# Attention before a mixture of experts: the second head pair's products in one run at the head of the next slot, ten score tiles in a row, router steps and sine products in other places

## The chip, the core and the metric

The kernel runs on one core of a Trainium2 chip. TensorE (PE) multiplies matrices and transposes, writing into PSUM; VectorE (DVE) and ScalarE (ACT) do the elementwise work and empty PSUM; GpSimd (POOL) does index work and indirect transfers; SyncE (SP) issues most DMA transfers. Each of them works through its own list in order, and they wait for each other on semaphores. The metric is the device time of one execution in microseconds (us), as a median of runs. Everything is in float32, except a small mask in bfloat16.

## The reference

Input x has the shape 8 x 1024 x 512 (batch, tokens, features). Two blocks follow each other, each on a layer norm of its input and each added to it. The second is a mixture of experts: a router (x @ Wr, softmax over 8 experts, the best 2, at most 160 tokens per expert and batch entry) and two matrix products per expert with a relu between. The change does not touch the experts. The first block is an attention with 16 heads of 32 features, whose queries, keys and values are sines and cosines of angles:

```python
theta_q = xh / (1.0 + jnp.abs(w_q)) + b_q + t * phi_q
sin_q, cos_q = lookup_sin_cos(theta_q)
Q = jnp.concatenate([cos_q, sin_q], axis=-1)          # the same for K
theta_v = xh / (1.0 + jnp.abs(w_v)) + b_v
V = cos_v + sin_v
scores = jnp.einsum('bqhd,bkhd->bhqk', Q, K) / scale
scores = jnp.where(causal, -jnp.inf, scores)
attn = jax.nn.softmax(scores, axis=-1)
out = jnp.einsum('bhqk,bkhd->bqhd', attn, V).reshape(B, S, D)
theta_out = out / (1.0 + jnp.abs(w_out)) + b_out
return cos_o + sin_o
```

`lookup_sin_cos` reads a table of 2048 steps with linear interpolation. A head's query and key vectors have 64 numbers (32 cosines and 32 sines).

## The kernel before

Attention is done in 32 slots, the loop `for n in range(NCK)` from line 1736. Slot n is batch entry b = n // 4 and feature block c = n % 4: 128 features, that is 4 heads, taken as two pairs of heads. A schedule written out by hand sets the order on PE, ACT, DVE and SP: the order in which Python emits instructions is the order on each of these engines. Most helpers are generators, and `some(k, gens)` and `rest(gen)` (lines 730 and 736) run so many steps of them, or all.

Scores. `scores` (line 675) makes ten tiles per pair of heads: three for the first 512 queries (h = 0) and seven for the second (h = 1). One tile holds the scores of 128 keys against 512 queries for both heads of the pair, two banks of PSUM; the two tiles of two blocks share one, and one tile per half is 256 wide. Line 684 are its matmuls (64 rows deep, the two heads side by side in the rows of the array), line 698 adds a causal mask to the tiles on the diagonal, and line 704 is the exponential on ACT, out of PSUM into an SBUF tile `e`. There are as many `e` buffers as one pair has tiles.

Products. `attend` (line 710) multiplies the exponentials of a tile with the values (line 718: 128 deep, 64 columns wide) and sums over the tiles in `av`, one bank; three steps for h = 0 and seven for h = 1. After the last step DVE copies `av` to `av_sb` (line 726). `turn` (line 742) transposes `av_sb` (PE, line 216), and DVE divides by the sums (lines 753 and 755).

Angles. For a slot two later, `qk_pre` (line 508) transposes x on PE (line 216) and DVE takes the angles out of PSUM in four steps (line 525). `angle` (line 437) shifts them on DVE; `both` (line 588) is two squares and two absolute values on ACT (lines 442 and 585); `qk_sin` (line 592) takes two sines on ACT (lines 594 and 445), behind a load of ACT's sine table, and the next exponential is behind a load of the other table. `qk_post` (line 599) makes the cosine products and the sine products on DVE (line 448, on `qk_c` and on `qk_r`), each followed by four DMAs from SP (line 609) that put them into the `qk` tiles of the two pairs. `v_pre` and `v_post` do the same for the values without transfers (lines 626, 631, 438, 448); `o_pre` and `o_post` for the attention's output (lines 647, 438, 448, 658, and the statistics of the next layer norm in line 661, together called `residual`). `layernorm1` normalizes the batch entry to come on DVE.

Router. `router` (line 787) is a generator for a finished batch entry; its steps are spread by hand over slots c = 0 to 3 of the next one. `next_rows` normalizes two tiles of rows on DVE and stores them, `features` transposes them on PE into a PSUM tile that DVE empties (line 838), `sums` multiplies by Wr (lines 858 and 875) and DVE empties it (lines 880 and 882); then come the choice of experts, and the places in the experts' lists. `route_on(k)` runs one step in slots with c = k.

PSUM. The pool `ps_s` has three buffers of two banks, given out in turn to score tiles, turns, `qk_pre`, and the router's `features`, `sums` and places. Whoever asks for the fourth waits until the first is emptied. `av` has two buffers of one bank. [...]

The order in one slot (away from the first and last): three steps of the second pair's h = 1 products of the slot before; in c = 1 `qk_pre`, `v_post`, a router step and `angle`; five score tiles of the first pair; the residual, the absolute values and the values' square; the last four steps of the products; the other five tiles; the second pair's turn of the slot before and `o_pre`; three steps of the first pair's products; sines; cosine products; seven steps of products; two score tiles of the second pair; the first pair's turn; sine products; three more tiles with the output's square before the last two; `qk_pre` in c = 1, 2, 3 (the router's start in c = 0); the second pair's h = 0 products; five tiles; the two squares.

Of the kernel before, what the change touches and what calls it, by code (L numbers as in the profile page):

```python
# [74 lines left out]
def preln_attn_moe_kernel(  # L75
# [424 lines left out]
    def load_base(n):  # L500
        if n < NCH:
            rest(make_base(n))
            return
        p = qkt.tile([P, 2, S], F32, name="qk_base")
        nc.sync.dma_start(p, base_d[n % NCH])
        bases[n] = p
# [157 lines left out]
    def tiles_of(h):  # L664


        def block(kb, at=0):
            q0 = max(512 * h, kb * P)
            return kb, q0, 512 * (h + 1) - q0, at

        d = 4 * h
        full = [[block(kb)] for kb in range(d + 1)]
        return full + [[block(d + 1), block(d + 3, 3 * P)], [block(d + 2)]]
# [36 lines left out]
    def attend(n, pr, h, es, halves):  # L710

        vt = v_tiles[n % 2]
        av = ps_av.tile([P, 512], F32, name="av")
        tiles = tiles_of(h)
        for i, parts in enumerate(tiles):
            for kb, q0, w, at in parts:
                for a in range(2):
                    nc.tensor.matmul(  # L718
                        av[a * 64 : (a + 1) * 64, q0 - 512 * h :],
                        lhsT=vt[:, kb, 2 * pr + a, :], rhs=es[i][:, a, at : at + w],  # L720
                        start=kb == 0, stop=i + 1 == len(tiles),
                    )
            if i + 1 == len(tiles):
                av_sb = avp.tile([P, 512], F32, name="av_sb")
                q = 2 * (n % NCH) + pr
                nc.vector.tensor_scalar(av_sb, av, inv_o[:, q : q + 1], None, ALU.mult)
                halves.append(av_sb)
            yield

    def some(count, *gens):  # L730

        for gen in gens:
            while count and next(gen, 0) is None:
                count -= 1

    def rest(gen):
        got = None
        for got in gen:
            pass
        return got  # L740
# [247 lines left out]
    def part(gen):  # L988

        for name in gen:  # L990
            if name is not None:
                return
            yield

    def keep(box, gen):
        for box[0] in gen:
            yield
# [82 lines left out]
    def find_rows(i):  # L1080

        js = slice(chunks[i][1], chunks[i][1] + 2 * chunks[i][2])
        lo, hi = REACH[i]
        nc.vector.tensor_scalar(
            source[:, :, js], meta[:, :, js, 0], float(hi * S), float(lo * S),
            ALU.min, ALU.subtract,
        )
# [542 lines left out]
    def experts_begin():  # L1630

        for name, bufs in (("gp", 2), ("w1p", 3), ("t1p", 3), ("xep", 1), ("tmp_p", 2)):
            pools[name] = to_end.pool(name, bufs, reuse_waits="tile", **right)
        for k in range(AHEAD):
            load_ahead(k)
        yield from start(first_gather, first_parts)
        mix_w1(0, 0)
# [76 lines left out]
    NCK = B * NCH  # L1714
# [10 lines left out]
    pairs, v_st = qk_first()  # L1725
# [5 lines left out]
    last = None  # L1731
    o_st = route = first_rows = None
    begin = False
    place, angles, residual = [None], iter(()), iter(())
    first_gather = gather(0)
    for n in range(NCK):
        more, late = n + 1 < NCK, last is not None
        b, c = divmod(n, NCH)
        if n == NCK - 1:
            to_inputs.close()  # L1740
            first_rows = experts_begin()
        pos_n = trig.tile([P, S], F32, name="o_p")
        if n == NCK - 2:
            find_rows(0)
            next(first_gather)
        if late:
            e11, halves1, pos = last
        es, halves = [[], []], [[], []]

        products = [attend(n, 0, h, es[h], halves[0]) for h in range(2)]
        if late:
            products.insert(0, attend(n - 1, 1, 1, e11, halves1))
        ahead = [scores(pairs[0], h, es[h]) for h in range(2)]
        v_box = [None]
        asides = [keep(v_box, v_pre(n + 1))] if more else [first_rows]
        if b == 0 and c in (1, 2):
            asides.append(layernorm1(1, c - 1))
        elif c == 0 and 0 < b < B - 1:  # L1760
            asides.append(layernorm1(b + 1, 1))
        elif c == 3 and b + 2 < B:
            asides.append(layernorm1(b + 2, 0))
        def route_on(slot):
            if c == slot and route is not None:
                next(route)

        def with_asides(count):
            for _ in range(count):
                some(1, *ahead)  # L1770
                for g in asides:
                    next(g, None)


        if late:
            some(3, *products)
        route_on(1)
        route_on(2)
        if c == 2 and route is not None:
            asides.append(part(route))  # L1780
        if n == 0:
            some(2, *ahead)
        if n == 0 or begin:

            qk_st = rest(qk_pre(n + 1))
            if begin:
                v_post(n, v_st)
                next(route)
            angle(*qk_st)
            angles = keep(place, both(qk_st))  # L1790
            if begin:
                load_base(n + 2)

        if begin:
            some(5, *ahead)
        else:
            with_asides(5)
        rest(residual)
        for _ in range(2):
            route_on(1)  # L1800
        rest(angles)
        if begin:
            rest(asides.pop(0))
            v_st = v_box[0]
        elif more:
            v_st = v_box[0]
            square(v_st[0])
        if late:
            some(4, *products)
        route_on(1)  # L1810
        route_on(1)
        with_asides(5)
        if begin:
            square(v_st[0])
        for g in asides:
            rest(g)
        if n == 0:
            magnitude(inv_o)
            base2 = make_base(2)
            next(base2)  # L1820
        if late:
            turn(1, halves1, pos)
            o_st = o_pre(n - 1, pos)
        route_on(1)
        route_on(1)
        if n == 2:
            load_b1()
        if c == 3 and b > 0:
            next(route)
            if b > 1:  # L1830
                fetch_slots(b - 2)
            if b < B - 1:
                scatter()


        some(3, *products)
        if n == 0:
            next(base2)
        if more:
            qk_st = place[0]  # L1840
            qk_sin(qk_st)
            sine(v_st[1])
        if late:
            sine(o_st[1])
        if n == 0:
            some(NTT, *products)
            rest(base2)
        if more:
            post = qk_post(qk_st)
            next(post)  # L1850
        some(NTT, *products)

        es, halves1 = [[], []], []
        ahead = [scores(pairs[1], h, es[h]) for h in range(2)]
        route_on(1)
        route_on(2)
        some(2, *ahead)
        turn(0, halves[0], pos_n)
        next_pairs = rest(post) if more else None
        some(1, *ahead)  # L1860
        if late:
            square(o_st[0])
            residual = o_post(n - 1, o_st)
        some(2, *ahead)
        begin = c == 0 and late
        if begin:
            rest(residual)
            route = router(b - 1)
            next(route)
        elif n + 2 < NCK:  # L1870
            route_on(1)
            qk_st = rest(qk_pre(n + 2))

        if c != 1:
            next(residual, None)
        if n + 2 < NCK and not begin and c != 1:
            angle(*qk_st)
        if c != 1:
            rest(residual)
        if c == 1:  # L1880
            load_mid(b)
        if c == 2 and b + 2 < B:
            load_x(b + 2)
        if more and not begin:
            v_post(n + 1, v_st)
        some(3, attend(n, 1, 0, es[0], halves1))
        route_on(1)
        if c == 1:

            angle(*qk_st)  # L1890
        some(5, *ahead)
        if n + 2 < NCK and not begin:
            angles = keep(place, both(qk_st))
            some(2, angles)
            if n + 3 < NCK:
                load_base(n + 3)
        last = (es[1], halves1, pos_n)
        pairs = next_pairs
    rest(attend(NCK - 1, 1, 1, es[1], halves1))
    turn(1, halves1, pos_n)  # L1900
    to_pairs.close()

# [57 lines left out]
```

## Time and profile before

| what | value |
|---|---|
| median of 3 runs | 3178.54 us (3177.48 to 3178.57) |
| the profiled execution | 3177.95 us |
| its span in the trace | 3176.2 us |
| PE busy, DVE busy, ACT busy | 3112.0, 2303.7, 1680.4 us |
| mean granted TensorE clock | 0.998 of full |
| L704 exponentials | 640, 569.4 us |
| L684 score matmuls | 3072, 598.3 us |
| L718 product matmuls | 3072, 523.4 us |

The span runs from the first instruction to the last. A busy engine is not always one that works: matmuls are pipelined, and their ends are modelled in the trace. A row of a timeline gives the start, the duration, the engine, the line, the operation with output and input, the form, how many were merged (x5), and in brackets how long the engine was idle before and what ended that. A row of the chain of waits gives the start, the length and what set the pace there.

### The profile page before, as it was taken

To read this page: it belongs to the slowest core of one execution; us is meant where nothing else is said; L and a number is where in the kernel's file an instruction comes from. 1 tells how busy PE (TensorE), PEld (TensorE's weight loads), DVE (VectorE), ACT (ScalarE), POOL (GpSimd) and SP (SyncE) were. 2 spreads that over 40 slices of the span, in tenths; PEclk is the share of its full clock that TensorE was granted. 3 is DMA by queue.
4 is the path that set the end of the run, shared out by engine and by line. 5 is a ranking of instruction groups with operands and counts; after the bars stand their busy time and mean duration, and the time that the engine had idled before them with its cause. 6 is when DMAs were issued, how large, how long until landed. Compare 5 with 4: busy or idle time off the path is not lost.

```text
span 3176.2 us, 52225 instructions
## 1 busy us (share of the span) xinstructions
PE 3112.0 (98%) x20086; PEld 2147.5 (68%) x20086; DVE 2303.7 (73%) x4808; ACT 1680.4 (53%) x2599; POOL 424.1 (13%) x387
## 2 busy tenths in 40 slices
PE   5999999999999999999999999999999999999998
PEld 2444444444444444689699699699698698698697
DVE  8888878887887775738658658658667767767765
ACT  7888888888888885413423423423423423423423
POOL 3000202020201122410110110110110110110010
PEclk9999999999999999999999999999999999999999
DMA  5535454555545352533523523523533433433421
GB/s 167 147 100 166 106 165 132 148 138 149 164 133 160 80 167 55 149 82 96 155 54 91 152 57 95 145 59 98 140 64 100 132 67 102 128 67 108 118 58 23
DMA packets 288552, 358.79 MB, mean 113 GB/s; under 512 B 28376, under 2 KB 199088, under 8 KB 276272
## 3 DMA queue, kind: packets, MB, share of 16 engines
q1 hardware_dynamic: 264944, 312.20, 33.7%
q0 software_dynamic: 22912, 43.22, 7.3%
q8 instruction: 160, 2.62, 0.4%
q14 instruction: 88, 0.72, 0.1%
q10 hardware_dynamic: 448, 0.02, 0.0%
HBM read 207.02 MB, written 81.22 MB: 91 GB/s over the span
## 4 chain that ended last, share of the span: by engine, by line
PE 78%; DVE 4%; ACT 1%; issue 1%; DMA 0%; SPq 0%; POOLq 0%; POOL 0%; DVEq 0%; ACTq 0%
PE ps_p L1238 30%; PE ps_p L1474 10%; PE ps_p L1537 10%; PE av L718 10%; PE ps_s L684 9%; PE ps_p L1352 8%; ACT e L704 1%; PE ps_s L216 1%; PE ps_s L698 1%; DVE qk_f L525 1%; DVE qk_r L448 0%; DMA qk<-qk_r 0%; DVE xT L838 0%; DVE xe L1174 0%; DVE xe_s L1186 0%
## 5 line engine op out<-in xcount | busy, mean ns | idle before, releaser
L704 ACT ACTIVATE e<-ps_s 128x1024 f32<-128x1024 f32 (+1 forms) x640 | 569.4, 937 | 183.5 <-PE ps_s L684 110.0
L684 PE MATMUL ps_s<-qk 64*128 64x512 f32 (+3 forms) x3072 | 598.3, 506 | 28.2 <-DMA qk<-qk_r 12.4
L718 PE MATMUL av<-e,v 128*64 128x512 f32 (+3 forms) x3072 | 523.4, 490 | 0.0
L684 PEld LDWEIGHTS ps_s<-qk 64*128 64x128 f32 x3072 | 262.3, 188 | 216.0 <-issue 106.9
L718 PEld LDWEIGHTS av<-e,v 128*64 128x64 f32 x3072 | 200.5, 137 | 283.0 <-issue 267.0
L1238 PE MATMUL ps_p<-xe,w 128*128 128x256 f32 (+1 forms) x1024 | 317.6, 433 | 1.1 <-issue 1.1
L1238 PE MATMUL ps_p<-xe_s,t 128*128 128x256 f32 (+1 forms) x1024 | 317.6, 433 | 0.0
L1238 PE MATMUL ps_p<-xe,t 128*128 128x256 f32 (+1 forms) x1024 | 317.6, 433 | 0.0
L1316 POOL DMA_INDIRECT out_dram<-y,slots x80 | 127.8, 1597 | 1261.3 <-ACT y L1311 1017.8
L769 POOL DMA_INDIRECT slot_d<-token,slot x128 | 156.6, 1223 | 997.3 <-issue 620.8
L1238 PEld LDWEIGHTS ps_p<-xe_s,t 128*128 128x128 f32 x1024 | 194.4, 190 | 81.4 <-issue 0.8
L1238 PEld LDWEIGHTS ps_p<-xe,t 128*128 128x128 f32 x1024 | 194.2, 190 | 80.4 <-issue 0.4
L1238 PEld LDWEIGHTS ps_p<-xe,w 128*128 128x128 f32 x1024 | 193.7, 190 | 79.4 <-issue 1.2
L1281 DVE TENSOR_TENSOR hid<-hid 128x256 f32<-128x256 f32 (+1 forms) x128 | 63.9, 499 | 206.4 <-ACT hid L1279 206.4
L1537 PE MATMUL ps_p<-w_t,hid 128*128 128x256 f32 x960 | 212.4, 379 | 0.8 <-DVE y L1590 0.8
L1537 PEld LDWEIGHTS ps_p<-w_t,hid 128*128 128x128 f32 x960 | 180.0, 190 | 24.4 <-DVE y L1590 1.2
L1238 PE MATMUL ps_p<-xe_s,w 128*128 128x256 f32 (+1 forms) x512 | 158.9, 433 | 0.6 <-ACT p L1254 0.6
L1352 PE MATMUL ps_p<-w,hid 128*128 128x256 f32 x640 | 142.9, 379 | 0.0
L1474 PE MATMUL ps_p<-w,hid 128*128 128x128 f32 x1104 | 141.8, 275 | 0.0
L698 PEld LDWEIGHTS <-keys_b 64*128 64x128 bf16 x1536 | 80.9, 95 | 89.7 <-issue 71.8
L1311 ACT ACTIVATE y<-y,slots 128x256 f32<-128x256 f32 (+1 forms) x120 | 65.9, 578 | 142.8 <-DVE y L1389 105.5
L1474 PEld LDWEIGHTS ps_p<-w,hid 128*128 128x128 f32 x1104 | 135.8, 192 | 2.3
(289 smaller groups left out, 5182.7 us busy)
## 6 DMA issues: line engine op xcount, KB each, us to landing
w<-in_L_ffn_W_dram SPq DMA_DIRECT2D x256, 256.0 KB, 3.4
w<-in_L_ffn_W_dram SPq DMA_DIRECT2D x64, 512.0 KB, 6.8
qk<-qk_c SPq DMA_DIRECT2D x124, 256.0 KB, 4.5
qk<-qk_r SPq DMA_DIRECT2D x120, 256.0 KB, 4.9
qk_base<-base_d SPq DMA_DIRECT2D x28, 1024.0 KB, 8.8
xn_d<-xn SPq DMA_DIRECT2D x72, 256.0 KB, 2.3
rows_d<-xg SPq DMA_DIRECT2D x70, 256.0 KB, 2.1
x_mid<-in_L_attn_x_dram SPq DMA_DIRECT2D x16, 1024.0 KB, 9.2
```

The lines of the kernel that those rows point to most:

```text
L684: nc.tensor.matmul(ps[:, a, at : at + w], lhsT=pair[r, 1, kb * P : (kb + 1) * P], rhs=pair[r, 0, q0 : q0 + w], start=at == 0, stop=not own ...
L698: nc.tensor.matmul(out_, lhsT=keys_b[r, part, :], rhs=late, start=False, stop=part == 1, skip_group_check=True,)
L704: nc.scalar.activation(e, ps[:, :, :n], AF.Exp, scale=UNIT * UNIT / math.sqrt(2 * DH))
L718: nc.tensor.matmul(av[a * 64 : (a + 1) * 64, q0 - 512 * h :], lhsT=vt[:, kb, 2 * pr + a, :], rhs=es[i][:, a, at : at + w], start=kb == 0, ...
L769: queued = nc.gpsimd.indirect_dma_start(out=slot_d[b], out_offset=bass.IndirectOffsetOnAxis(ap=idx, axis=0), in_=src, in_offset=None,)
L1238: nc.tensor.matmul(ps, lhsT=weights[:, k, :], rhs=rows[:, k, :], start=first and k == 0, stop=last and k == 1, skip_group_check=True,)
L1281: TT(g1, g3, h22, ALU.add)
L1311: nc.scalar.activation(part, part, AF.Identity, scale=meta[:, e, jj[r], 1:2].bitcast(F32))
L1316: ins = nc.gpsimd.indirect_dma_start(out=out, out_offset=bass.IndirectOffsetOnAxis(ap=meta[:, e, jj[r], 0:1], axis=0), in_=y, in_offset=No ...
L1352: nc.tensor.matmul(ps, lhsT=hid[:, k, part, cols], rhs=ws[weight][:, k, :], start=first and k == 0, stop=last and k == NHQ - 1, skip_group ...
L1474: nc.tensor.matmul(ps, lhsT=left[:, k, :], rhs=right[:, k, :], start=first and k == 0, stop=k == 3, skip_group_check=True,)
L1537: nc.tensor.matmul(ps[:, b * DC : (b + 1) * DC], lhsT=hid[:, k, part, b * P : (b + 1) * P], rhs=ws[weight][:, k, :], start=first and k == ...
```

## The change

The h = 0 products of the second pair, which stood among that pair's own scores, and the two parts of its h = 1 products, which stood around the first five score tiles of the next slot, become one run of ten steps at the head of the next slot. So each pair's ten score tiles follow each other with no products between (turns, `qk_pre` and router steps still stand among them). The rest of `angles` (absolute values; in c = 1 squares too) comes after the first three steps of that run. In c = 1 `qk_pre`, `v_post`, `angle` and the load of the next base come before the run, and the router steps that stood at the head follow it; two router steps stand after the seventh score tile instead of after the old four product steps. The sine products with their four DMAs come straight after the first pair's products, before the router steps and the turn. In c = 1 `angle` comes before the second pair's last five tiles instead of after a product run. Every computation is still there, in the same number.

```diff
@@ -1743,15 +1743,14 @@
         if n == NCK - 2:
             find_rows(0)
             next(first_gather)
-        if late:
-            e11, halves1, pos = last
         es, halves = [[], []], [[], []]
 
 
 
         products = [attend(n, 0, h, es[h], halves[0]) for h in range(2)]
         if late:
-            products.insert(0, attend(n - 1, 1, 1, e11, halves1))
+            es1, halves1, pos = last
+            products = [attend(n - 1, 1, h, es1[h], halves1) for h in range(2)] + products
         ahead = [scores(pairs[0], h, es[h]) for h in range(2)]
         v_box = [None]
         asides = [keep(v_box, v_pre(n + 1))] if more else [first_rows]
@@ -1772,12 +1771,6 @@
                     next(g, None)
 
 
-        if late:
-            some(3, *products)
-        route_on(1)
-        route_on(2)
-        if c == 2 and route is not None:
-            asides.append(part(route))
         if n == 0:
             some(2, *ahead)
         if n == 0 or begin:
@@ -1785,11 +1778,19 @@
             qk_st = rest(qk_pre(n + 1))
             if begin:
                 v_post(n, v_st)
-                next(route)
             angle(*qk_st)
             angles = keep(place, both(qk_st))
             if begin:
                 load_base(n + 2)
+        if late:
+            some(3, *products)
+            rest(angles)
+            some(7, *products)
+        for _ in range(2):
+            route_on(1)
+        route_on(2)
+        if c == 2 and route is not None:
+            asides.append(part(route))
 
         if begin:
             some(5, *ahead)
@@ -1805,11 +1806,10 @@
         elif more:
             v_st = v_box[0]
             square(v_st[0])
-        if late:
-            some(4, *products)
-        route_on(1)
-        route_on(1)
-        with_asides(5)
+        with_asides(2)
+        for _ in range(2):
+            route_on(1)
+        with_asides(3)
         if begin:
             square(v_st[0])
         for g in asides:
@@ -1849,14 +1849,14 @@
             post = qk_post(qk_st)
             next(post)
         some(NTT, *products)
-
-        es, halves1 = [[], []], []
-        ahead = [scores(pairs[1], h, es[h]) for h in range(2)]
+        next_pairs = rest(post) if more else None
+
+        es1, halves1 = [[], []], []
+        ahead = [scores(pairs[1], h, es1[h]) for h in range(2)]
         route_on(1)
         route_on(2)
         some(2, *ahead)
         turn(0, halves[0], pos_n)
-        next_pairs = rest(post) if more else None
         some(1, *ahead)
         if late:
             square(o_st[0])
@@ -1883,20 +1883,21 @@
             load_x(b + 2)
         if more and not begin:
             v_post(n + 1, v_st)
-        some(3, attend(n, 1, 0, es[0], halves1))
+        if c == 1:
+
+            angle(*qk_st)
+        some(3, *ahead)
         route_on(1)
-        if c == 1:
-
-            angle(*qk_st)
-        some(5, *ahead)
+        some(2, *ahead)
         if n + 2 < NCK and not begin:
             angles = keep(place, both(qk_st))
             some(2, angles)
             if n + 3 < NCK:
                 load_base(n + 3)
-        last = (es[1], halves1, pos_n)
+        last = (es1, halves1, pos_n)
         pairs = next_pairs
-    rest(attend(NCK - 1, 1, 1, es[1], halves1))
+    for h in range(2):
+        rest(attend(NCK - 1, 1, h, es1[h], halves1))
     turn(1, halves1, pos_n)
     to_pairs.close()
 
```

More of the change, by code (lines that the diff above doesn't have):

```diff
@@ L1885, in preln_attn_moe_kernel @@
             v_post(n + 1, v_st)
-        some(3, attend(n, 1, 0, es[0], halves1))
-        route_on(1)
         if c == 1:
             angle(*qk_st)
-        some(5, *ahead)
+        some(3, *ahead)
+        route_on(1)
+        some(2, *ahead)
         if n + 2 < NCK and not begin:
```

## The prediction

> **What bounds the kernel now.** First the page, for the engines' shares and the clock.
>
> ```profile
> PE 3112.0 (98%) x20086; PEld 2147.5 (68%) x20086; DVE 2303.7 (73%) x4808; ACT 1680.4 (53%) x2599; POOL 424.1 (13%) x387
> PEclk9999999999999999999999999999999999999999
> ```
>
> TensorE sets the time and its clock is full, so only its work and its waits count. The change stays within attention (about the first 1250 us). Next, busy time per slot of one batch, each stretch running from one ten-step product run to the next (c=0, 1, 2, 3):
>
> ```profile
> 807.51:848.14 40.63, 39.78 (x372) 19.96 (x368) 33.19 (x69) 32.02 (x34) 12.67 (x12) 1.00 0.56 156
> 848.14:887.46 39.32, 38.59 (x372) 19.13 (x368) 30.43 (x62) 32.54 (x34) 0.00 (x0) 1.00 0.67 216
> 887.46:923.70 36.24, 36.19 (x308) 17.84 (x304) 30.94 (x66) 31.89 (x33) 0.00 (x0) 1.00 0.51 146
> 923.70:959.64 35.94, 35.89 (x292) 17.61 (x289) 29.95 (x62) 31.76 (x33) 10.23 (x8) 1.00 0.38 89
> ```
>
> The columns after the stretch are its length, then PE, PEld, DVE, ACT and POOL busy. In c=2 and c=3 PE is idle for 0.05 us: hardly any wait is left to remove. ACT and DVE are busy for 30 to 32 of 36 us: little cover if their work is squeezed. The chain in such a slot:
>
> ```profile
> 923.77 7.89 PE av L718 x48
> ...
> 933.93 1.03 ACT e L704
> ...
> 937.49 2.30 PE av L718 x16
> 939.80 2.77 PE ps_s L684 x12
> ...
> 944.26 2.73 PE av L718 x12
> ...
> 951.58 3.16 PE av L718 x20
> ```
>
> The first pair's products are one run of 7.89 us; the second pair's are three, 2.30, 2.73 and 3.16. Twelve L684 matmuls are three full score tiles, so PE makes a tile in 0.93 us. The ACT piece shows three PSUM buffers just falling short: PE waits for an exponential about 0.3 us. ACT and DVE beside it:
>
> ```profile
> 912.35 4.46 ACT L704 ACTIVATE e<-ps_s 128x1024 f32<-128x1024 f32 x5 [0.33 <-PE ps_s L698]
> 916.70 2.01 ACT L585 ACTIVATE qk_c<-qk_r 128x1024 f32<-128x1024 int32 x2
> 918.60 1.15 ACT L442 ACTIVATE v_p<-v_p,split_c 128x1024 f32<-128x1024 uint16 x1
> 919.97 4.39 ACT L704 ACTIVATE e<-ps_s 128x1024 f32<-128x1024 f32 x5 [0.23 <-PE ps_s L684]
> ```
> ```profile
> 934.43 0.26 DVE L753 RECIPROCAL rec<-ps_s 128x16 f32<-128x16 f32 x1 [1.96 <-PE ps_s L216]
> 935.33 2.28 DVE L448 SCALAR_TENSOR_TENSOR qk_r<-qk_f,qk_r 128x2048 f32<-128x2048 f32 x1
> 937.71 2.73 DVE L525 SCALAR_TENSOR_TENSOR qk_f<-ps_s,inv_qk,qk_base 128x512 int32<-128x512 f32 x4
> 945.13 1.23 DVE L438 TENSOR_SCALAR qk_r<-qk_f 128x2048 int32<-128x2048 int32 x1 [2.30 <-DMA qk<-qk_r]
> ```
>
> Five tiles of exponentials take ACT 4.4 us (a full one 0.945), about PE's own 4.5 for five tiles. What lets ACT do 3.1 us of other work (L585, L442) between fives is the 3.16 us of products that PE does there. On DVE, qk_pre's evacuation (L525) holds a PSUM buffer for about 3 us after its transposes; PE has the 2.30 us product run to pass that in.
>
> **The change, part by part.** Times are on one slot, from the start of the run named.
>
> (1) One product run in place of three: 2.30+2.73+3.16 = 8.19 becomes 7.89. Gain 0.30 per slot. The Trainium skill, "TensorEngine Tiling (Array Packing)", section Key Properties, says that changing the tiling mode drains the array; products and scores differ in shape (128*64 against 64*128), and the row's price is 0.15 per cut. The same page, section PSUM Bottleneck, speaks against the change: faster tiled matmuls move the limit to evacuation. By the first rule alone the sum is -0.30 a slot; the rows say that the second governs a long run, as follows.
>
> (2) First pair's ten scores in a row. The L585 pair moves under the head's product run, but the v square (L442, 1.04 in the queue) stays between fives, and PE no longer pauses. ACT starts at 1.31 (912.35-911.04) and ends five exponentials at 5.7, the square at 6.75, then exponentials 6, 7, 8 at 7.75, 8.7, 9.65. PE unhindered would start tile 9 at 4.54+3x0.93 = 7.33; it takes the buffer of tile 6, so 7.8: 0.45 late. The turn's transposes take tile 8's buffer at 9.7 instead of 9.4: 0.3 to 0.4 more. Loss 0.85. Bounds: 0.3 (only the tile 9 wait, partly), 1.3 (the square itself waits for DVE's angle, due at about 5.7 too).
>
> (3) Second pair's scores without the 2.30 products. The buffers rotate tile 1, 2, turn, 3, 4, 5, qk_pre, 6, 7, 8. As now, tile 4 starts at 3.4, tile 5 ends at 5.25, qk_pre at 5.85. Tiles 6 and 7 follow exponentials 4 and 5, which end at 5.95 and 6.9 now (the o square and two exponentials run to 938.46, less 931.60) and end at 6.95 and 7.9. Tile 8 wants qk_pre's buffer, free at 6.05+2.73 = 8.8: it waits 0.95. End of tile 10 at 11.4; now the same work takes 944.19-931.60-2.30 = 10.3. Loss 1.1 (bounds 0.3 and 1.5). It applies where qk_pre stands there: c=1, 2, 3 up to slot 29.
>
> (4) The sine products (L448 on qk_r, 2.28) go ahead of the first pair's turn. Their time is hidden in DVE's idle 1.96 before L753; the turn's evacuation ends at 4.05 instead of 3.7, before tile 5 needs it at 4.35. The four DMAs leave some 3 us sooner, so the 2.30 us angle wait disappears, but DVE alone gains by that. No other SP transfer is passed. What is late next: router steps that used to come before them on DVE, items 5 and 6.
>
> (5) c=1 with a router (7 slots). Head: qk_pre, then 7.89 of products, cover DVE's backlog (residual 4.1, statistics and rows 4.5, after the turn's 4.05: until 12.6 of a run whose tile 10 ends at 10, so 2.6 into the head; then 2.7, 1.2 and 1.2), which now costs stalls:
>
> ```profile
> 834.97 1.99 PE L684 MATMUL ps_s<-qk 64*128 64x512 f32 x8 [0.56 <-DVE qk_f L525]
> ```
>
> From head to the turn's end now 20.7+2.30 = 23.0; after 0.9 (qk_pre) +7.9+0.7 (features) + ten tiles with three router buffers and the turn, 12.9 with about 1.1 of waits: 22.4. Gain 0.6. The two row stores move behind a qk_base load on SP; both are needed only slots later. Second pair: the logits' buffer is evacuated behind the sine products, at 3.7 instead of 1.5, and the turn needs it at 2.85: 0.85. Then features and qk_pre hold two buffers for 1.3+2.7 with no product run between; tile 8 waits 1.05; exponential waits add 0.7. Total waits about 2.7 against 1.1 now: loss 1.6. Net loss 1.0 (bounds -1 and +3).
>
> (6) c=2 with a router (7 slots). DVE is busy from v's first product at 874.89 to the second pair's turn at 888.49, 13.6 us; ten scores and a turn on PE take 10.4 after the head. With one evacuation taken out (it now comes first) DVE reaches the turn 13.7 after the head, three late. Turn 0.95, o work 1.9, evacuation 0.7 and cosine products 2.28 bring it to 19.5; the products end at 10.65+7.9 = 18.55, so their evacuation is done at 20.2, the sine products at 22.4, the router's places (0.95, before the sine products until now) at 23.3. The places, PE's first work after the products, took the buffer that the turn of the first pair is to have, at 18.55+0.6+2.1 = 21.3: 2.1 late. Net loss of the slot 0.85+1.1+2.1-0.3 = 3.8 (bounds 1.6, if DVE catches up, and 5.5).
>
> (7) c=0 gets (1) and (2): +0.55. Moved angle in c=1: DVE alone, under products.
>
> Sum: nine ordinary slots (c=3 of batches 0 to 6, c=1 and 2 of batch 0) at 0.85+1.1-0.30 = 1.65: 14.9. Slot 31 0.55; seven c=0 3.9; seven c=1 7.0; six c=2 22.8, slot 30 2.7. Total 51.8. The profiled execution is 3177.95 (span 3176.2 and 1.75 around it), 0.6 below the median of 3178.54: forecast 3177.95+52 = 3230. The feed-forward stage keeps its order.
>
> **Rivals.** *Only ACT binds* (0.17): DVE's buffers come free in time because PE is already late by exponentials. Then 0.55 for 31 slots, 17: 3195. For it: exponentials 4 and 5 nearly hold tiles 6 and 7. Against: the 0.56 wait above is DVE's with this very buffer.
>
> *DVE runs behind throughout router slots* (0.15): c=1 +3 and c=2 +5.5 give 14.9+0.6+3.9+21+36 = 76: 3254. For it: 13.7 into 10.4. Against: the eight us of products at each head let DVE catch up.
>
> *The cut's price decides, faster* (0.14): where exponentials and evacuations come free before PE asks, 31 times 0.30 is left, 9.3: 3169. It decides from the point where the waits of a slot fall below 0.30 in total, which needs tile 9 and tile 8 to be less than 0.15 late each. For it: PE's 0.93 and ACT's 0.945 are close and ACT's lag at the head is cleared. Against: the square's 1.04 is in the middle, and ends at both limits are worked from rows.
>
> *Gains and waits cancel* (0.06): about 3178.
>
> **How the numbers follow.** My case has 0.48, within 3205 to 3258. The range leaves out the faster case and most of the cancelling one: 3190 to 3258. Chances, with 0.2% (6.4 us) about what a measurement of this kernel can tell: slower 0.48+0.17+0.15 = 0.80, same 0.06, faster 0.14.
>
> **What would show it.** (1) products of 7.89 us twice per slot. (2) PE waiting for ACT e at the ninth tile and the turn. (3) a PE wait on DVE qk_f in c=2 and c=3, which is absent now, and periods of 37.6 for c=3. (4) no DVE wait for DMA qk<-qk_r. (6) DVE's first-pair turn late in c=2, period about 40. The prediction is wrong if slots keep their 36 us: then the buffers are free earlier than I reckon, or PE's 0.93 grows in long runs and leaves ACT time.

## The result and the profile after

The changed kernel takes 3250.57 us (median of 4 runs, 3249.84 to 3250.82) against 3178.01 for the kernel before beside it: a ratio of 1.0229, with a 95% interval of 1.0211 to 1.0246. It is slower by 72.6 us. That lies inside the range (3190 to 3258) and is on the forecast side, but some 21 us above the forecast of 3230. The profiled span is 3248.6 us against 3176.2, and all of the difference is in attention: the first L1238 matmul (the first product of the experts) starts at 1332.2 us instead of 1259.7.

The four slots of one batch entry, in the windows view of the changed kernel (the columns are those of the view before; c=0, 1, 2, 3). They belong to batch entry 4, those shown before to entry 5; before the change, slots of one c differ by less than 0.5 us between entries 1 to 6:

```profile
692.97:737.14 44.17, 41.12 (x372) 20.23 (x369) 33.34 (x70) 31.77 (x34) 8.94 (x10) 0.96 0.38 102
737.14:778.19 41.05, 39.01 (x372) 19.39 (x369) 29.10 (x52) 32.01 (x33) 0.00 (x0) 1.00 0.62 201
778.19:817.67 39.48, 36.51 (x308) 18.11 (x304) 32.03 (x76) 31.59 (x33) 0.00 (x0) 1.00 0.46 134
817.67:855.92 38.25, 36.36 (x293) 17.86 (x289) 30.58 (x64) 31.81 (x33) 12.06 (x9) 1.00 0.34 84
```

The slots that took 40.63, 39.32, 36.24 and 35.94 take 44.17, 41.05, 39.48 and 38.25. PE's idle time in c=3 has gone from 0.05 to 1.89 us, and the clock, the third number from the end, is not full in the first row. What PE waits for from 100 to 1330 us, in the waits view of the changed kernel (total us, times, longest):

```profile
PE ps_s L684 <- ACT e L704: 47.9, 80, 1.6
PE ps_s L216 <- DVE tmp L966: 12.2, 7, 1.8
PE ps_s L216 <- DVE prob L882: 4.4, 7, 0.6
```

Before, the first of these rows had 1.1 us, and the other two were absent. No row of this stretch names DVE qk_f, though step (3) of the prediction expected one. The chain of an ordinary slot (c=3), from the first pair's products to the product run at the next slot's head, shows what comes first instead:

```profile
654.79 7.89 PE av L718 x48
...
663.90 1.06 ACT L704
...
665.20 1.95 ACT e L704 x2
...
674.90 7.89 PE av L718 x48
```

The 1.06 us piece is no exponential. In the timeline of ScalarE it has a name:

```profile
663.90 1.28 ACT L704 ACT_TABLE_LOAD   x1 [1.47 <-PE ps_s L698]
665.20 2.56 ACT L704 ACTIVATE e<-ps_s 128x1024 f32<-128x1024 f32 x3
```

ACT is done with its sines and idle for 1.47 us, but the load of the exponential's table waits for TensorE's first score tile, and the exponential stands behind it. In a slot of c=3 of the kernel before, the load began before the products had ended (931.66) and was over at 932.67, just ahead of the end of the first score tile (932.81):

```profile
931.39 1.28 ACT L704 ACT_TABLE_LOAD   x1
932.85 2.75 ACT L704 ACTIVATE e<-ps_s 128x1024 f32<-128x1024 f32 x3 [0.17 <-PE ps_s L698]
```

Of the 33 loads that stand before an exponential, one waited for PE before the change and 31 do after it. The waits view has them as the row of L704 without a tile, first before, then after:

```profile
ACT L704 <- PE ps_s L698: 4.7, 1, 4.7
ACT L704 <- PE ps_s L698: 54.9, 31, 4.7
```

The built program shows what differs. Where the first exponential has two semaphores to wait for (PE's, and that of an earlier instruction of ACT itself), the wait for PE is an instruction of its own, and it stands in front of the table load. Where it has only PE's, the exponential carries the wait and nothing stands in front of the load.

Below, the period of a slot is the time from the start of its first pair's products to the start of the next slot's. A slot's second half runs from the start of its first pair's products to the product run at the next slot's head; a slot's head runs from that product run to its own first pair's products. So a period is the second half of one slot and the head of the next. Differences in us are ratios to the kernel before run on the same chip, times 3178, since the chips' own level differs (the kernel before took 3177 beside the first four experiments, 3190 and 3191 beside the others). The traces give a second measure, the time of the first L1238 matmul, at which attention ends. For e1 to e4 it agrees with the ratio within 2 us. For e5 to e12, on the other chips, it puts the run 2 to 8 us later than the ratio does; no trace of the kernel before was kept there, so a few us carry no weight in these runs.

### The profile page after: what moved, and what is told of

It is laid out like the page before. It is cut to its first block, busy times and chain, and to the rows that moved or that the text cites. A ratio compares the mean times of both kernels' runs of the same rounds, so it can differ in the third digit from the quotient of the medians.

```text
span 3248.6 us, 52378 instructions
## 1 busy us (share of the span) xinstructions
PE 3124.2 (96%) x20086; PEld 2153.8 (66%) x20086; DVE 2305.9 (71%) x4808; ACT 1673.2 (52%) x2599; POOL 421.1 (13%) x387
## 4 chain that ended last, share of the span: by engine, by line
PE 76%; DVE 11%; ACT 9%; issue 3%; DMA 0%; ACTq 0%; POOLq 0%; POOL 0%; DVEq 0%
PE ps_p L1238 30%; PE av L718 11%; PE ps_p L1474 10%; PE ps_p L1537 9%; PE ps_p L1352 7%; PE ps_s L684 6%; ACT e L704 6%; PE ps_s L216 1%; ACT L704 1%; DVE st_mid L661 1%; DVE qk_f L525 1%; ACT o_p L442 1%; DVE qk_r L448 1%; PE ps_s L698 1%; DVE x_mid L658 1%
## 5 line engine op out<-in xcount | busy, mean ns | idle before, releaser
L704 ACT ACTIVATE e<-ps_s 128x1024 f32<-128x1024 f32 (+1 forms) x640 | 563.8, 944 | 161.4 <-PE ps_s L698 124.9
L718 PE MATMUL av<-e,v 128*64 128x512 f32 (+3 forms) x3072 | 509.5, 488 | 0.0
L1238 PE MATMUL ps_p<-xe_s,t 128*128 128x256 f32 (+1 forms) x1024 | 317.7, 433 | 0.0
L1238 PE MATMUL ps_p<-xe,t 128*128 128x256 f32 (+1 forms) x1024 | 317.6, 433 | 0.0
L1238 PE MATMUL ps_p<-xe,w 128*128 128x256 f32 (+1 forms) x1024 | 317.6, 433 | 0.0
L1238 PEld LDWEIGHTS ps_p<-xe_s,t 128*128 128x128 f32 x1024 | 194.4, 190 | 81.4 <-issue 0.8
L1238 PEld LDWEIGHTS ps_p<-xe,t 128*128 128x128 f32 x1024 | 194.2, 190 | 80.4 <-issue 0.4
L1238 PEld LDWEIGHTS ps_p<-xe,w 128*128 128x128 f32 x1024 | 193.7, 190 | 78.2
L726 DVE TENSOR_SCALAR av_sb<-av,inv_o 128x512 f32<-128x512 f32 x128 | 95.1, 747 | 124.6 <-PE av L718 124.1
L1238 PE MATMUL ps_p<-xe_s,w 128*128 128x256 f32 (+1 forms) x512 | 158.9, 433 | 0.6 <-ACT p L1254 0.6
L698 PEld LDWEIGHTS <-keys_b 64*128 64x128 bf16 x1536 | 79.7, 95 | 90.3 <-issue 72.6
```

The source lines that it names most:

```text
L698: nc.tensor.matmul(out_, lhsT=keys_b[r, part, :], rhs=late, start=False, stop=part == 1, skip_group_check=True,)
L704: nc.scalar.activation(e, ps[:, :, :n], AF.Exp, scale=UNIT * UNIT / math.sqrt(2 * DH))
L718: nc.tensor.matmul(av[a * 64 : (a + 1) * 64, q0 - 512 * h :], lhsT=vt[:, kb, 2 * pr + a, :], rhs=es[i][:, a, at : at + w], start=kb == 0, ...
L1238: nc.tensor.matmul(ps, lhsT=weights[:, k, :], rhs=rows[:, k, :], start=first and k == 0, stop=last and k == 1, skip_group_check=True,)
```

## The experiments

**e1: the table loaded early.** A tiny exponential after the sines takes the load, away from the score tile.

```diff
             sine(o_st[1])
+        nc.scalar.activation(warm, split_c, AF.Exp)
```

> The changed kernel plus one exponential of a 128x1 tile on ScalarE straight after the sines (line 1845), so that the exponential's table is loaded there and not at the second pair's first score tile, where the load now waits for TensorE (1.47 us idle before it). Theory A (after the load, the PSUM buffer that qk_pre holds is next in line, as the forecast had it): about 0.4 us less in the second-pair half of c=2 and c=3, 0.9 in c=0, 1 at the head of c=1, together some 15 us less than the changed kernel's 3250: 3235, and waits of TensorE for DVE qk_f appear. Theory B (the late load alone sets the second-pair half): 1.2 us in each of 31 slots, 37 us: 3213.

Measured: 3227.98 us, ratio 1.0159 (1.0142 to 1.0176), 22 us less than the changed kernel. The second half of c=3 falls from 20.11 to 19.02, of c=0 from 19.34 to 18.25; of c=2 from 21.34 to 20.75 and of c=1 only from 22.56 to 22.32. So the late load costs 1.1 us where nothing else waits; theory B is right on that and wrong on the rest (22 us in all, not 37). What remains in c=3 against before is 0.83 us (19.02-7.89 = 11.13, where the same work took 10.30), and it is not what theory A says either:

```profile
658.38 2.04 PE L684 MATMUL ps_s<-qk 64*128 64x512 f32 x8
660.70 1.13 PE L684 MATMUL ps_s<-qk 64*128 64x512 f32 x4 [0.27 <-ACT e L704]
```
```profile
658.32 2.72 DVE L525 SCALAR_TENSOR_TENSOR qk_f<-ps_s,inv_qk,qk_base 128x512 int32<-128x512 f32 x4 [2.04 <-PE ps_s L216]
```

Tile 8 (the second row of PE) starts at 660.70, before DVE's evacuation of qk_pre ends at 661.04, and just after an exponential (tile 6's, at about 660.64). So it does not take qk_pre's buffer, as the prediction had it, but tile 6's: while qk_pre holds one of three buffers, two are left to circulate.

**e2: the absolute values back between the fives**, in slots that do not begin a router.

```diff
             some(3, *products)
-            rest(angles)
+            if begin:
+                rest(angles)
             some(7, *products)
```

> The changed kernel with the two absolute values (line 585, 2.0 us) back between the first pair's first five score tiles and the rest in every slot that does not begin a router. Theory A (ScalarE holds the ten-run of the first pair): 2.0 us more in 24 slots, less 0.4 because the table load no longer carries a wait there: about +38, 3288. Theory B (the wait on the table load was what the moved absolute values cost, and the ten-run has room): 1.2 us less in 24 slots, 3221.

Measured: 3286.17 us, ratio 1.0346 (1.0329 to 1.0363), 37 us more. Both theories' mechanisms are there, with A's far larger: the head of c=3 and c=0 goes from 18.14 to 20.0 or more (+1.9: ScalarE holds the ten-run), and the second half of c=3 from 20.11 to 18.96 (-1.15: the table load waits for PE in 8 of 33 places now). That these come so near to theory A's 38 is in part luck: the second halves win some 19 us in all, and in eleven of the longer heads the clock falls as well (last section), which adds some 12 us that theory A did not have. Moving the absolute values away from the ten-run is needed, and it is also what made the table load wait.

**e3: in c=1 the squares and absolute values after the first five**, as before the change.

```diff
             some(3, *products)
-            rest(angles)
+            if not begin:
+                rest(angles)
             some(7, *products)
```

> The changed kernel, but in c=1 with a router the squares and absolute values come after the first five score tiles, as before the change. Theory A (at this head ScalarE stands behind the DVE's late angle, and three buffers fill while it does): 2 to 3 us less in each of 7 slots, and where TensorE no longer idles 1.6 us its clock does not fall: together 15 to 25 less, 3225 to 3235. Theory B (DVE's evacuations hold that head, whatever ScalarE does): within 3 us of 3250.

Measured: 3252.99 us, ratio 1.0238 (1.0221 to 1.0255), no less than the changed kernel. Theory A falls. The first five tiles do go through, but then TensorE waits 2.31 us before the eighth tile for exponentials queued behind the same 4 us of ScalarE work. The work has to stand somewhere in this head, and neither of the two places tried is free.

**e4: the sine products back behind the turn.**

```diff
-        next_pairs = rest(post) if more else None
...
         turn(0, halves[0], pos_n)
+        next_pairs = rest(post) if more else None
```

> The changed kernel with the sine products back behind the first pair's turn. Theory A (forecast step 6: in c=2 and c=1 the router's buffer is emptied behind the sine products and the turn waits for it): 2.1 us less in 7 slots c=2, 0.6 to 0.9 in 7 slots c=1, about 20 less: 3230, and the waits of TensorE for DVE tmp and DVE prob go. Theory B (waits for exponentials take their place): 0 to 5 less.

Measured: 3238.93 us, ratio 1.0193 (1.0176 to 1.0210), 11 us less. The waits for DVE tmp and for DVE prob at the turn are gone, but the second half of c=2 falls by 0.87 only (21.34 to 20.47), that of c=1 not at all, and waits for exponentials grow from 47.9 to 57.4 us in the profiled execution. The remaining 5 us are falls of the clock that this execution did not have (last section). In between the theories: the wait is real, and more than half of it would have been spent on the next one.

**e5: the second pair's h = 0 products back among its scores.**

```diff
-            products = [attend(n - 1, 1, h, es1[h], halves1) for h in range(2)] + products
+            products = [attend(n - 1, 1, 1, es1[1], halves1)] + products
...
-            some(7, *products)
+            some(4, *products)
...
             v_post(n + 1, v_st)
+        some(3, attend(n, 1, 0, es1[0], halves1))
...
```

> The changed kernel with the three h = 0 product steps of the second pair back behind qk_pre, between that pair's own scores (the head's run is seven steps). Theory A (forecast step 3: tile 8 waits for the buffer that qk_pre holds): 1.1 less 0.15 for the new cut in 23 slots, 22 less than 3250: 3228. Theory B (the late table load already holds TensorE before qk_pre, so only the 0.6 us that the changed kernel's trace shows behind qk_pre can be won): 0.45 in 23 slots, 10 less: 3240.

Measured: ratio 1.0197 (1.0180 to 1.0214), 10 us less (7 by the trace), as theory B has it. The period of c=3 falls by 0.6, that of c=2 by 0.95 and that of c=1 by 0.7, while the period from c=0 to c=1, with c=1's head in it, is 0.7 longer (43.3 against 42.6, where neither kernel has a fall of the clock); the run of products in that head is shorter. Step (3)'s 1.1 is not won while the table load is late.

**e6: the last four product steps back between the first pair's fives.**

```diff
-            some(7, *products)
+            some(3, *products)
...
             square(v_st[0])
+        if late:
+            some(4, *products)
         with_asides(2)
```

> The changed kernel with the last four product steps of the head back between the first pair's two fives. Theory A (forecast step 2: ScalarE holds the ten-run, at tile 9 and at the turn): 0.85 less 0.15 for the cut in 24 slots, 17; and in 7 slots c=1 with a router, where ScalarE's angle work stands before the run, 2 to 3 more and no falls of the clock, 14 to 25: together 3208 to 3220. Theory B (the exponentials are late by as much at the next stage, so the wait moves): within 5 us of 3250.

Measured: ratio 1.0257 (1.0240 to 1.0274), 9 us more (13 by the trace). In ordinary slots theory A holds: the head of c=3 is 17.54 instead of 18.14. At c=1's head it fails badly; the period from c=0 to c=1 is 47.3 to 48.0 instead of 42.6 to 44.5:

```profile
725.16 1.22 PE L684 MATMUL ps_s<-qk 64*128 64x256 f32 x4 [2.71 <-DVE xT L838]
728.24 3.74 PE L684 MATMUL ps_s<-qk 64*128 64x512 f32 x8 [1.70 <-ACT e L704]
...
733.12 3.23 PE L718 MATMUL av<-e,v 128*64 128x512 f32 x20
```

The products at 733.12 are the cover that was taken away; without them PE reaches the scores sooner, and waits first for DVE, then for ScalarE. A part of the loss is the clock: in each of these seven heads it is half for 6.83 us, in the changed kernel for 3.41 us in three of them (last section). At this head the chain of DVE's backlog, the angle, and ScalarE's squares and absolute values sets the time in this run; TensorE's earlier start only lengthened its wait.

**e7: the values' square after the ten tiles.**

```diff
             v_st = v_box[0]
-            square(v_st[0])
         with_asides(2)
...
         with_asides(3)
-        if begin:
+        if more:
             square(v_st[0])
```

> The changed kernel with the values' square (line 442, 1.04 us in ScalarE's queue) after the ten score tiles and not between five and five. Theory A (with that square out, ScalarE's 0.945 a tile nearly keeps TensorE's 0.93): 0.7 less in 24 slots, 17: 3233. Theory B (three buffers are too few for a ten-run even so): 0 to 4 less.

Measured: ratio 1.0179 (1.0162 to 1.0196), 16 us less; but in the trace attention ends only 7 us sooner (1324.9 against 1332.2), so the total does not tell the theories apart. The slots do, for theory A. The heads of c=2, 3 and 0 lose 0.95 to 1.0 us each (18.14 to 17.19): the square in the middle was nearly the whole of TensorE's wait in the ten-run, and three buffers are enough without it. But c=2 pays 2.0 us in its second half:

```profile
621.19 1.12 PE L216 MATMUL ps_s<-ident,av_sb 64*128 64x64 f32 x16 [2.77 <-DVE tmp L966]
```

DVE is no faster, so the turn waits the longer for the buffer of the places: 2.77 us instead of 1.74. The rest of the 2.0 goes with a fall of the clock behind this wait, in all seven slots.

**e8: the sine products alone**, in the kernel before.

```diff
         some(NTT, *products)
+        next_pairs = rest(post) if more else None
...
         turn(0, halves[0], pos_n)
-        next_pairs = rest(post) if more else None
```

> The kernel before, with one part of the change alone: the sine products straight after the first pair's products. Theory A (hidden in DVE's idle 1.96 in slots without router work, but the router's buffer is emptied behind them and the turn waits for it): 1.3 more in 7 slots c=2, 0.8 in 7 slots c=1, 0 elsewhere: about +14, 3192. Theory B (there is slack enough everywhere): within 3 us of 3177.

Measured: ratio 1.0028 (1.0017 to 1.0038), 9 us more (13 by the trace), theory A: the periods of c=2 grow by 1.15, of c=1 by 0.57, and c=3 and c=0 do not change.

**e9: three losses taken out together**, the edits of e1, e4 and e7 in one kernel.

> The changed kernel with three of its losses taken out together: the early exponential of a 128x1 tile, the sine products back behind the turn, and the values' square after the ten tiles. Theory A (they are separate terms): 22 (early table) + 11 (sine) + 22 (0.95 at 23 heads; the 2 us that this square cost in c=2 came through the sine products and goes with them): 55 of the 73 us, ratio to the kernel before 1.0055. Theory B (one wait passes to the next): no more than 35 us, ratio 1.012.

Measured: ratio 1.0093 (1.0077 to 1.0108), 43 of the 73 us recovered (39 by the trace), between the theories. The periods of c=1 and c=2 come to 38.93 and 37.35, but that of c=3 only to 36.92: its second half is 19.72 here against 19.02 in e1. ScalarE is the cause. In this slot the products start at 634.25:

```profile
634.80 1.15 ACT L442 ACTIVATE v_p<-v_p,split_c 128x1024 f32<-128x1024 uint16 x1
635.97 1.28 ACT L594 ACT_TABLE_LOAD   x1
```
```profile
645.43 0.70 PE L684 MATMUL ps_s<-qk 64*128 64x256 f32 x4 [0.50 <-ACT e L704]
```

The values' square, moved behind the ten tiles by e7's edit, now stands just ahead of the sines. Their table load begins 1.72 us after the products' start instead of 0.72 (e1), the exponentials are later by nearly as much, and TensorE waits for one at the third tile, where e1 has no wait. The late table load had hidden this in e7, whose second half of c=3 is 20.11, as in the changed kernel.

**e10: the absolute values alone**, ahead of the first five tiles in the kernel before.

```diff
         if late:
             some(3, *products)
+            rest(angles)
```

> The kernel before with one part of the change alone: the absolute values (line 585) ahead of the first five score tiles. Theory A (this move makes the second pair's first exponential need two waits, one of which the table load in front of it then carries, so that the load starts only with the first score tile): 1.1 us in 24 slots, 26: ratio 1.008. Theory B (the late load comes from the ten-runs): within 0.1% of the kernel before.

**e11: the same with the early exponential** of e1.

> The same as e10_abs_alone plus the early exponential of a 128x1 tile. Theory A (the late table load is all that the moved absolute values cost): back to the kernel before, plus up to 0.2 us a slot for the added exponential: ratio 1.000 to 1.002. Theory B (absolute values ahead of the scores delay the exponentials themselves): 1.004 or more.

Measured: e10 1.0128 (1.0113 to 1.0144), e11 1.0077 (1.0061 to 1.0092). In e10 the waits view has 24 table loads that wait for PE, against one in the kernel before, and in c=2 the second half up to the h = 0 products grows from 14.08 to 15.25; in e11 it is back at 14.14. So this move by itself makes the load late, and 1.1 us is its price in the second half of such a slot; over the whole kernel, e11 takes 16 us less than e10 (13 by the trace). The rest of e10 and all of e11 is theory B's, here in e11:

```profile
780.13 2.04 PE L684 MATMUL ps_s<-qk 64*128 64x512 f32 x8 [1.40 <-ACT e L704]
```

With only three product steps ahead of the scores, squares and absolute values (4 us, until 779.08 in this slot) still run when the first tiles are ready, and TensorE waits for the exponentials behind them; the changed kernel's ten steps do cover them.

**e12: a try at a better kernel before**, two of the four product steps ahead of the first five tiles in c=1.

```diff
         if begin:
+            some(2, *products)
             some(5, *ahead)
...
-            some(4, *products)
+            some(2 if begin else 4, *products)
```

> The kernel before, but in c=1 with a router two of the four product steps stand ahead of the first five score tiles, as cover for the evacuation of features and qk_pre that now costs TensorE about 1 us there. Theory A: 0.9 less 0.15 for a new cut in 7 slots, 5 us: ratio 0.9985. Theory B (the angle work on ScalarE then meets the second five): no gain, 1.000 to 1.002.

Measured: ratio 0.9993 (0.9986 to 0.9999). In the trace the c=0 periods, which hold this head, are no shorter (40.56 to 41.22, against 40.63 to 40.87). If there is a gain it is at most 0.14%, the lower end of the interval, and the trace shows none: attention ends at 1259.9, against 1259.7 before. No version run here clearly beats the kernel before.

## Why the prediction was right, and where not

The direction and most of the size follow from what was reckoned: the second pair's products in one run win 0.30 us a slot, and what the cuts had covered comes back as waits. But the total came nearer than its parts. Steps (3) and (5) put 24 us on a wait for qk_pre's buffer that did not come (1.1 in 15 slots, 1.05 in 7), and a wait that no step looked for, the late table load, cost 22 us (e1): that these two are alike is luck. By period, summed over all slots, forecast against the traces:

| period (slots summed) | forecast, us | measured, us |
|---|---|---|
| batch 0 (4) | 5 | 8.5 |
| c=0 to c=1, with c=1's head (7) | -4 | 18.9 |
| c=1 to c=2 (7) | 15 | 12.1 |
| c=2 to c=3 (6, router batches but the last) | 22.5 | 19.5 |
| c=3 to c=0 (6) | 10 | 13.6 |
| what is left at the end | 3 | 0 |

(1) Right. Both product runs take 7.89 us. That the 0.15 per cut is the drain named in the Trainium skill, "TensorEngine Tiling (Array Packing)", section Key Properties, and not some other cost of starting a run, no run here shows. What the prediction took from the same page, section PSUM Bottleneck, is said there of matmuls that tiling has made faster, and as what may happen. Here no matmul got faster (48 products take 7.89 us before and after); what bound was ScalarE, once the products between the score tiles were gone.

(2) Right in mechanism and nearly in size. The loss was put at 0.85 less 0.30 a head. The head of c=3, with seven product steps, took 15.45; with the 2.30 of the three steps that moved into it, 17.75. It takes 18.14: +0.39, against +0.55. The wait at the ninth tile, put at 0.45, is there, in the head at which the chain above ends:

```profile
690.50 1.14 PE L684 MATMUL ps_s<-qk 64*128 64x384 f32 x8 [0.52 <-ACT e L704]
```

e7 finds 0.95 for the square alone.

(3) Wrong in mechanism, low in size. It put 1.1 us on tile 8 waiting for qk_pre's buffer. The second half of c=3 lost 1.92 (18.19 without the 2.30 products before, 20.11 after), and its period is 38.25, not 37.6. Of the 1.92, 1.1 is the table load that waits for TensorE (e1, e2), a wait that the step did not look for: it let the sines' block with its two loads (8.3 us, from 924.38 to 932.67 in the kernel before) end where it ended before. The other 0.83 are waits for exponentials while two buffers circulate (the rows shown at e1); tile 8 does not take the buffer named.

(4) Right on the cost: hidden in c=3 and c=0 (e8). The angle's DMA wait, which was to disappear, is shorter but not gone: 17.1 us in 11 waits, against 42.1 in 21.

(5) The step that was furthest off. It forecast 1.6 lost in c=1's second half, where 1.3 were, and a gain of 0.6 us at c=1's head (22.4 instead of 23.0). The period from c=0 to c=1 lost 1.9 to 3.9 instead. Of the 23 us between -4 and 18.9, 7.7 are seven late table loads in c=0's second half, and some 5 are three falls of the clock. The remaining 10 or so are the head itself, 1.5 in each: with qk_pre's 0.64 it takes 23.9 to 24.2 where the clock does not fall. The step started DVE's residual work at 4.05, right after the turn, while it waits for ScalarE's square of the output:

```profile
707.08 1.23 DVE L448 SCALAR_TENSOR_TENSOR t_r<-o_p,t_r 128x1024 f32<-128x1024 f32 x1 [2.26 <-ACT o_p L442]
```
```profile
720.52 2.19 ACT L442 ACTIVATE qk_f<-qk_f,split_c 128x1024 f32<-128x1024 uint16 x2 [7.50 <-DVE qk_r L438]
724.51 2.40 ACT L704 ACTIVATE e<-ps_s 128x1024 f32<-128x1024 f32 x3
```

That is 6.2 us after the products, not 4.05; the late table load, ahead of the square on ScalarE, is 1.1 of it (5.1 in e1). Everything behind it on DVE is late with it, the angle ends at 720.5, and the squares and absolute values keep the exponentials until 724.5, when TensorE has been at its scores since 720.75. Neither the other place for that ScalarE work (e3) nor TensorE's other order (e6) shortened the head.

(6) Right in mechanism, high in size: the turn waits for the buffer of the places (12.2 us in seven waits, 1.7 each against 2.1), and e4 wins 0.87 of it when the order is undone, since exponentials are next. The period of c=2 is 39.48, near the 40 named, but 0.6 of that is the late table load (e1), which the step did not have.

The rival *only ACT binds* (3195) has the right name on the waits but too small a price. *DVE runs behind* (3254) gives nearly the measured time, for another reason: it put 36 us on c=2, where the change lost about 20. The rival *faster* needed less than 0.30 of waits in a slot; PE is idle for 1.9 to 3.05 in each of the four slots shown.

What stays open: why the exponential has a second semaphore to wait for after the absolute values have moved. The built instructions show that it does; no run shows that the wait is needed.

## What to carry to other kernels

Product runs between score tiles look like cuts that cost 0.15 us each, but they were the time in which two other engines caught up; before joining them, list each engine's work between two runs and see that it fits without the gap. A table load can be held up by the wait of the activation behind it: where a block of sines is followed by exponentials, look whether the row of the load has idle time ended by another engine (31 such rows cost 22 us here), or give the load a tiny activation of its own (0.20 us here). When a chain over other engines (DVE's backlog, the angle, ScalarE) sets a stage, giving the matmul engine a shorter way to it lengthens the wait (e6).

## What the runs showed of the hardware

The granted clock of TensorE falls after idle stretches of under 3 us. One-microsecond windows of the changed kernel around the 1.62 us wait of c=1's head (PE's busy time is the number after the comma; the clock is the third from the end):

```profile
724.00:725.00 1.00, 0.00 (x0) 0.00 (x0) 0.00 (x0) 1.00 (x2) 0.00 (x0) 1.00 0.71 259
725.00:726.00 1.00, 0.43 (x2) 0.30 (x4) 0.00 (x0) 1.00 (x2) 0.00 (x0) 1.00 0.72 275
726.00:727.00 1.00, 1.00 (x6) 0.52 (x4) 0.00 (x0) 0.91 (x2) 0.00 (x0) 0.64 0.00 0
727.00:728.00 1.00, 1.00 (x4) 0.11 (x2) 0.00 (x0) 0.92 (x1) 0.00 (x0) 0.50 0.00 0
...
729.00:730.00 1.00, 1.00 (x19) 0.37 (x12) 0.23 (x1) 0.81 (x1) 0.00 (x0) 0.65 0.00 0
```

The clock is half for 3.41 us (from 726.28), so 1.71 us of work is lost, about as much again as the wait; c=1's heads with a fall are 1.3 to 1.9 us longer than those without. In the profiled executions this happened after the 1.6 us waits at c=1's head in 3 of 7 cases of the changed kernel, in none of 7 in e4 and e7 and in 4 of 7 in e9. With 2.31 us there (e3) it came 5 times of 7. After the 2.77 us waits of c=2 in e7 it came 7 times of 7, and in e6, with 2.71 and 1.70 close together, 7 of 7 for 6.8 us each. In the kernel before, where no wait of these slots reaches 1 us, it did not happen once between 70 us and the last 10 us. The length of the wait alone does not decide: in c=2 of the changed kernel TensorE waits 1.74 us for the buffer of the places, in seven slots, and the clock stayed full after each. A wait near 1.6 us at c=1's head thus has two prices, 1.6 or some 3.3, and which one is paid differs from slot to slot; what decides it, these runs do not show.
